# A gated delta-net block with FFN on one core: first norm and gates moved among the slots, FFN moved into the attention's buffers, substitution steps moved behind x0

## The chip, the core and the metric

The kernel runs on one core of a Trainium2 chip. The metric is the device time of one execution in microseconds. TensorE is called PE, VectorE DVE, ScalarE ACT, GpSimd POOL and SyncE SP; SP issues all DMAs here. Everything is computed in float32.

## What is computed

The input x has 4 sequences of 1024 tokens with 256 features. The reference, cut to what matters:

```python
x = x + layernorm(attn(layernorm(x)))
x = x + layernorm(ffn(layernorm(x)))

# attn: gated delta rule, 32 value heads on 16 key heads of width 128, chunks of C = 64 tokens
mixed = silu(conv4(x @ W_qkv.T)); q, k, v = split(mixed); q, k = l2norm(q), l2norm(k)
beta  = sigmoid(x @ W_b.T)
g     = -exp(A_log) * softplus(x @ W_a.T + dt_bias);  gc = cumsum(g) in each chunk
decay = exp(gc_i - gc_j) for i >= j
A     = -((beta*k) @ k.T * decay) below the diagonal
T     = inverse(I - A)                       # unit lower triangular, 64 x 64
u, kcd = T @ (beta*v), T @ (beta*k*exp(gc))
for each chunk in order, with the state S (128 x 128 per head):
    v_new = u - kcd @ S
    out   = (q*exp(gc)) @ S + (q @ k.T * decay) @ v_new
    S     = S*exp(gc_last) + (k*exp(gc_last - gc)).T @ v_new
attn = (out * rsqrt(mean(out^2)) * norm_w * silu(x @ W_z.T)) @ W_out.T

# ffn: weights are looked up, w = lut[idx] with 16 entries; inner width 688
ffn = (silu(x @ Wg.T) * (x @ Wu.T)) @ Wd.T
```

## The kernel before

A *tile* is 128 tokens: the same chunk of two sequences (names `ab`). A *unit* of the attention is one tile for one *group* of 4 value heads (2 key heads). There are 32 tiles and 8 groups, so 256 units. Eight units make a *super*; there are 32 supers, four to a group.

**Head.** The first norm runs over four blocks of eight tiles (L207): load x, statistics (`layer_norm_stats`, DVE with the root on POOL), scale (`normed_to`), transpose on PE into `xnT` (all normed tokens, features on the partitions), and multiply by the weights of beta and g into `ba`. Then the gates of all heads are computed on 128x1024 tensors (L225 to L256), and for each group `dk` (exponentials of the sums, the sums, beta, the decay of a chunk) goes to DRAM as `dk_d`, the sums by rows as `rows_d` (L258 to L280). `load_qk` brings `dk` back when its group begins.

**Slots.** The attention is a software pipeline whose order on PE, ACT, DVE and POOL is written out by hand: every engine executes its instructions in the order of the program. Slot s, from -21 to 255, runs a list of names from `SLOTS`, chosen by the index iq = (s + 21) mod 8:

- `B`, `A`: one channel of q/k (for units 21 slots ahead) and one of v (4 slots ahead): PE products `pp` into a two-bank PSUM tile (two of these exist, shared by `A`, `B` and the state product `pu`), ACT gives the first tap into `cv`, DVE the other three taps (L439), ACT the SiLU.
- `n`, `s`: norms of q and k; scores with the decay (`kkq`, `dc`, `lT`, `aT`).
- `v1`: one step of `invert`, a forward substitution over 31 columns for all 32-row diagonal blocks of a super: a product into `rank` (L579) and a subtraction from `v` (L580), both DVE with two inputs in SBUF. The 31 steps of a super are dealt out over eight slots. `b` (`build`) makes the other blocks; `expand` loads the result into `ue`, `ae`.
- `N0` to `N3`, then `O3`, `O4`, `J` one slot later: the steps of a unit. `N0` transposes v (`pv`) into x0; `N1` multiplies by the state (`pkqs`), and DVE adds the result to x0 (L694); `N2` applies the inverse to x0 (PE `px`, L703), ACT and DVE evacuate (`xs`, `yg`), POOL decays the state (L720); `O3` gives the output of the chunk (`po`, `core`); `O4` is the state product `pu` and its addition to S (L747); `J` squares on ACT.
- `Z`, `T`, `U`: the output projection (`project_out`) of a unit five slots back: `pz` on PE, SiLU on ACT, two products on POOL (L783, L785), transposes, `pout`, and the sum over groups through `acc_d` in DRAM.

After `O4` one step of the lookup of the FFN's weights runs on POOL (`pieces`, L300 and L304).

**Tail.** After slot 255 five projections run one after another; the pools of the attention close; the FFN (L931) loads its weights and goes over four blocks of eight tiles: second norm, gate and up (`pgu`), product `hT`, down (`py`), last norm, store.

Of the kernel before, what the change touches and what calls it, by code (L numbers as in the profile page):

```python
# [2 lines left out]

# [55 lines left out]
def bc(ap, shape):  # L59
    return ap.to_broadcast(shape)  # L60
# [3 lines left out]
def delta_net_ffn_kernel(  # L64
# [43 lines left out]
    ones = filled("ones", 1.0, BS)  # L108
# [18 lines left out]
    nc.sync.dma_start(cw, convw)  # L127
    nw = const.tile([P, 1], F32, name="nw")
    nc.sync.dma_start(nw, normw)
    lutb = const.tile([P, NLUT], F32, name="lutb")  # L130
    nc.sync.dma_start(lutb, lut.to_broadcast([P, NLUT]))
# [24 lines left out]
    dk_d = dram.tile([NG, P, DK], F32, name="dk_d")  # L156
    rows_d = dram.tile([NG, 2, NTILE * HG, C], F32, name="rows_d")

    def rows_of(t, n0, n, p, ab):

        r = (2 * p + ab) * S + n0 * C
        return t[r : r + n * C, :].rearrange("(n t) d -> t n d", t=C)

    def tile_rows(xt, p, ab):

        return xt.rearrange("q (n p) d -> q n p d", p=NPAIR)[ab * C : (ab + 1) * C, :, p, :]
# [15 lines left out]

    def transposed(dst, srcs):

        for kc in range(KC):
            pt = bank("pt")
            for i, src in enumerate(srcs):
                T_.transpose(pt[:, i * P : (i + 1) * P], src[:, kc * P : (kc + 1) * P], ident)
            to = dst(kc)
            A.copy(to, pt if len(to.shape) == 2 else pt.rearrange("p (n b t) -> p n b t", n=2, b=B))  # L190


    with tc.tile_pool(name="pre", bufs=2) as pre, tc.tile_pool(name="gates", bufs=1) as gp:
        wb = gp.tile([P, KC, 2 * NV], F32, name="wb")
        nc.sync.dma_start(wb, wba.rearrange("(c p) n -> p c n", p=P))
        dtr = gp.tile([P, NV], F32, name="dtr")
        nc.sync.dma_start(dtr, dtb.to_broadcast([P, NV]))
        nea = gp.tile([P, NV], F32, name="nea")
        nc.sync.dma_start(nea, alog.to_broadcast([P, NV]))
        ba = gp.tile([P, NTILE, 2 * NV], F32, name="ba")  # L200
        sel = []
        for ab in range(2):
            rows = gp.tile([P, P], F32, name=f"sel{ab}")
            G_.memset(rows, 0.0)
            G_.memset(rows[ab * C : (ab + 1) * C, :], 1.0)
            sel.append(rows)
        for s in range(NSB):  # L207
            xt = pre.tile([P, SB, HID], F32, name="xt")
            for p in range(NPAIR):
                for ab in range(2):  # L210
                    nc.sync.dma_start(tile_rows(xt, p, ab), rows_of(x, 4 * s, 4, p, ab))
            mv, r = layer_norm_stats(pre, lambda i: xt[:, i, :], SB, "a")
            for i in range(SB):
                normed_to(xt[:, i, :], xt[:, i, :], mv, r, i)
            for h in range(2):
                at = H + (4 * s + 2 * h) * C
                transposed(
                    lambda kc: xnT[:, kc, :, at : at + BT].rearrange("p b (n t) -> p n b t", n=2),
                    [xt[:, 4 * h + i, :] for i in range(4)],
                )  # L220
            pg = bank("pg")
            for i in range(SB):
                by_rows(pg[:, i * 64 : (i + 1) * 64], lambda kc: wb[:, kc, :], s * SB + i)
            A.copy(ba[:, s * SB : (s + 1) * SB, :], pg.rearrange("p (t n) -> p t n", n=64))
        full = [P, NTILE, NV]  # L225
        gl = gp.tile(full, F32, name="gl")
        beta = gp.tile(full, F32, name="beta")
        A.activation(beta, ba[:, :, 0:NV], AF.Sigmoid)
        A.activation(nea, nea, AF.Exp)
        V.tensor_scalar_mul(nea, nea, -1.0)  # L230
        y = gp.tile(full, F32, name="y")
        u = gp.tile(full, F32, name="u")
        w = gp.tile(full, F32, name="w")
        d = gp.tile(full, F32, name="d")
        l = gp.tile(full, F32, name="l")
        V.tensor_tensor(y, ba[:, :, NV:], bc(dtr.unsqueeze(1), full), ALU.add)


        A.activation(u, y, AF.Abs)
        A.activation(u, u, AF.Exp, scale=-1.0)  # L240
        V.tensor_scalar_add(w, u, 1.0)
        A.activation(l, w, AF.Ln)
        V.tensor_scalar(d, w, -1.0, LOG1P_SERIES / 2, ALU.add, ALU.max)
        V.reciprocal(d, d)
        V.tensor_mul(l, l, d)
        V.tensor_mul(l, l, u)
        V.tensor_scalar(w, u, -1 / 4, 1 / 3, ALU.mult, ALU.add)
        V.tensor_mul(w, w, u)
        V.scalar_tensor_tensor(w, w, -1 / 2, u, ALU.add, ALU.mult)
        V.scalar_tensor_tensor(w, w, 1.0, u, ALU.add, ALU.mult)  # L250
        V.tensor_sub(l, l, w)
        V.scalar_tensor_tensor(l, u, LOG1P_SERIES, l, ALU.is_gt, ALU.mult)
        V.tensor_add(l, l, w)
        V.tensor_scalar_max(y, y, 0.0)
        V.tensor_add(y, y, l)
        V.tensor_tensor(gl, y, bc(nea.unsqueeze(1), full), ALU.mult)  # L256
        nth = NTILE * HG
        for g in range(NG):  # L258
            hs = slice(g * HG, (g + 1) * HG)
            dk = pre.tile([P, DK], F32, tag="dk", name="dk")  # L260
            ps = bank("pgate")
            for i, lhs in enumerate((triu, slow)):
                T_.matmul(ps[:, i * nth : (i + 1) * nth], lhsT=lhs, rhs=gl[:, :, hs], start=True, stop=True)
            A.activation(dk[:, 0 : 2 * nth], ps[:, 0 : 2 * nth], AF.Exp)
            V.tensor_copy(dk[:, 2 * nth : 3 * nth], ps[:, 0:nth])
            ps = bank("pgate")
            for ab in range(2):
                T_.matmul(
                    ps[:, ab * nth : (ab + 1) * nth], lhsT=sel[ab], rhs=gl[:, :, hs], start=True, stop=True
                )  # L270
            el = dk[:, 4 * nth : 6 * nth].rearrange("p (t a h) -> p a t h", a=2, h=HG)
            A.activation(el, ps[:, 0 : 2 * nth].rearrange("p (a t h) -> p a t h", a=2, h=HG), AF.Exp)
            V.tensor_copy(dk[:, 3 * nth : 4 * nth].rearrange("p (t h) -> p t h", h=HG), beta[:, :, hs])
            ps = bank("prow")
            T_.transpose(ps[:, :P], dk[:, 2 * nth : 3 * nth], ident)
            rows = pre.tile([P, P], F32, tag="rows", name="rows")
            A.copy(rows, ps[:, :P])
            for ab in range(2):
                nc.sync.dma_start(rows_d[g, ab], rows[:, ab * C : (ab + 1) * C])
            nc.sync.dma_start(dk_d[g], dk)  # L280
# [27 lines left out]
    with ExitStack() as main:  # L308
# [17 lines left out]
        for name in ("ue", "ae"):  # L326
            zeroed[name] = [w1.tile(h4, F32, tag=f"{name}{i}", name=name) for i in range(NZ)]
            for t in zeroed[name]:
                G_.memset(t, 0.0)
# [3 lines left out]
        for t in pads:  # L333
            G_.memset(t, 0.0)
# [706 lines left out]
```

## Time and profile before

| | |
|---|---|
| median of 3 runs | 4435.06 us (4429.75 to 4438.18) |
| execution profiled | 4434.46 us, of which span 4432.7 us |
| granted clock of PE in it | 0.968 |
| first norm done, by its last products | 55 us |
| first channel product (slot -21) | 109.7 us |
| first transposes of v (slot 0) | 254 us |
| last unit's output (slot 255) | 4017 us |
| first instruction of the FFN's second norm | 4097.5 us |

The profile is one execution. A row of a stage table gives start:end, length, and the busy time of PE, of PE's weight loads, of DVE, ACT and POOL in it, each with its number of instructions, then the granted clock of PE, the DMA share and GB/s. Matmuls are pipelined, so a busy PE is not a PE at its peak. A line of the timeline gives start, length, engine, line, operation, what is written and read, and in brackets the idle time of the engine ahead of it and what ended it. Every matmul in float32 shows as two instructions.

### The profile page before, as it was taken

The numbers are of one execution on the slowest core, as the hardware profiler recorded it, in microseconds if no ns is written. First come the engines' busy times: TensorE is split into PE (matmuls) and PEld (weight loads), VectorE is DVE, ScalarE is ACT, GpSimd is POOL, SyncE is SP. The second block draws the span as 40 slices with busy tenths as digits, with TensorE's granted clock in tenths as the row PEclk, the third lists the DMA queues.
The fourth block names the chain that finished last, engine by engine and source line by source line (L and its number), as shares of the span: only waits on it lengthen the run. The fifth ranks groups of instructions, "written<-read, shape, count | busy, mean of one in ns | idle before, by whom it ended". The sixth has DMA issues, their size and how long they took to land.

```text
span 4432.7 us, 79363 instructions
## 1 busy us (share of the span) xinstructions
PE 4021.3 (91%) x26664; PEld 2876.3 (65%) x26664; DVE 3514.5 (79%) x6641; ACT 2646.0 (60%) x6573; POOL 2069.1 (47%) x1752
## 2 busy tenths in 40 slices
PE   3679999999999999999999999999999999995888
PEld 3456766676767766677667676776766666673444
DVE  4788888888888888888888888889888888861442
ACT  2466666666666666666666666666666666662111
POOL 2545554655555555554455555555453334331221
PEclk7899999999999999999999999999999999997999
DMA  3444444544454444444444445444444444432110
GB/s 94 114 116 110 106 120 118 133 117 114 129 135 125 118 121 132 114 116 127 126 130 118 115 127 135 125 116 118 126 119 117 123 126 120 102 84 72 36 33 19
DMA packets 1052418, 492.70 MB, mean 111 GB/s; under 512 B 729824, under 2 KB 951152, under 8 KB 1052016
## 3 DMA queue, kind: packets, MB, share of 16 engines
q1 hardware_dynamic: 1052016, 487.64, 42.0%
q8 instruction: 216, 3.54, 0.3%
q14 instruction: 186, 1.52, 0.1%
HBM read 267.66 MB, written 219.69 MB: 110 GB/s over the span
## 4 chain that ended last, share of the span: by engine, by line
PE 59%; DVE 24%; issue 6%; ACT 6%; POOL 3%; DMA 2%; SPq 1%; DVEq 0%; POOLq 0%; ACTq 0%
PE pp L422 13%; DVE cv L439 8%; PE pout L796 7%; PE pz L142 7%; PE pkqs L683 7%; PE px L703 4%; DVE rank L579 4%; PE pu L740 4%; PE po L703 3%; PE pgu L963 3%; PE py L975 2%; DVE v L580 2%; PE kkq L545 2%; PE pto L789 2%; PE pv L670 1%
## 5 line engine op out<-in xcount | busy, mean ns | idle before, releaser
L439 DVE SCALAR_TENSOR_TENSOR cv<-pp,cw,cv 128x512 f32<-128x512 f32 x1536 | 1148.8, 748 | 356.6 <-ACT cv L436 327.2
L783 POOL TENSOR_TENSOR zs<-zs,rr 128x512 f32<-128x512 f32 x256 | 266.4, 1041 | 1586.6 <-ACT zs L781 1577.6
L436 ACT ACTIVATE cv<-pp,cw 128x512 f32<-128x512 f32 x512 | 350.7, 685 | 489.3 <-PE pp L422 489.3
L580 DVE TENSOR_TENSOR v<-v,rank 128x31 f32<-128x31 f32 (+15 forms) x992 | 555.0, 559 | 34.1
L422 PE MATMUL pp<-xnT,wq 128*128 128x262 f32 x2048 | 532.1, 402 | 43.8 <-DVE cv L439 35.1
L796 PE MATMUL pout<-wo,oT 128*128 128x256 f32 x2048 | 512.0, 395 | 8.1 <-ACT oT L791 8.1
L422 PEld LDWEIGHTS pp<-xnT,wq 128*128 128x128 f32 x2048 | 372.7, 192 | 217.1 <-issue 59.6
L422 PE MATMUL pp<-xnT,wv 128*128 128x262 f32 x2048 | 502.5, 387 | 6.1 <-DVE cv L439 6.1
L142 PE MATMUL pz<-wzs,xnT 128*64 128x512 f32 x2048 | 488.8, 598 | 4.7 <-DVE ac L801 3.8
L579 DVE TENSOR_TENSOR rank<-v,lb 128x31 f32<-128x31 f32 (+15 forms) x992 | 468.2, 472 | 24.5 <-DMA lb<-ltd 18.8
L683 PE MATMUL pkqs<-S,qku 128*64 128x256 f32 x3840 | 476.8, 387 | 4.2 <-DVE core L727 2.5
L720 POOL TENSOR_TENSOR S<-S,dkm 128x1024 f32<-128x1024 f32 x224 | 436.2, 1947 | 26.0 <-PE pkqs L683 26.0
L703 PE MATMUL px<-x,ue 128*128 128x128 f32 x2048 | 296.1, 289 | 157.5 <-issue 102.2
L703 PEld LDWEIGHTS px<-x,ue 128*128 128x128 f32 x2048 | 266.9, 196 | 258.0 <-issue 147.7
L422 PEld LDWEIGHTS pp<-xnT,wv 128*128 128x128 f32 x2048 | 381.4, 190 | 74.1 <-issue 13.4
L796 PEld LDWEIGHTS pout<-wo,oT 128*128 128x128 f32 x2048 | 388.2, 200 | 56.3 <-ACT oT L791 10.0
L683 PEld LDWEIGHTS pkqs<-S,qku 128*64 128x64 f32 x3840 | 249.2, 136 | 201.4 <-issue 51.0
L732 ACT ACTIVATE junk<-core 128x128 f32<-128x128 f32 x1024 | 318.8, 311 | 66.7 <-DVE core L727 38.4
L785 POOL TENSOR_TENSOR zs<-zs,core 128x512 f32<-128x512 f32 x256 | 328.4, 1283 | 20.1
L708 ACT ACTIVATE xs<-px 128x512 f32<-128x512 f32 x256 | 154.4, 603 | 237.5 <-PE px L703 237.4
L740 PE MATMUL pu<-yg,kt 64*128 64x256 f32 x1920 | 272.2, 402 | 15.4 <-DVE cv L439 14.0
L300 POOL TENSOR_SCALAR lt<-lx,lutb 128x344 f32<-128x344 int32 (+2 forms) x210 | 276.6, 1317 | 16.9
(166 smaller groups left out, 7081.7 us busy)
## 6 DMA issues: line engine op xcount, KB each, us to landing
qkd<-qk SPq DMA_DIRECT2D x256, 256.0 KB, 2.5
qku<-qkd SPq DMA_DIRECT2D x256, 256.0 KB, 2.9
dc<-rows_d SPq DMA_DIRECT2D x256, 128.0 KB, 3.4
ltd<-lT SPq DMA_DIRECT2D x128, 256.0 KB, 2.5
atd<-aT SPq DMA_DIRECT2D x128, 256.0 KB, 2.8
ae<-atd SPq DMA_DIRECT2D x512, 64.0 KB, 2.6
acc_d<-ac SPq DMA_DIRECT2D x256, 128.0 KB, 2.2
ac<-acc_d SPq DMA_DIRECT2D x224, 128.0 KB, 2.6
```

Source lines behind the costliest of these rows:

```text
L142: T_.matmul(ps[ab * C : (ab + 1) * C, :], lhsT=xnT[:, kc, 2 * p + ab, H + n * C : H + (n + 1) * C], rhs=rhs(kc), start=kc == 0, stop=kc == ...
L422: T_.matmul(ps[:, 2 * p : 2 * p + 2, : H + BT], lhsT=wt[:, kc, :], rhs=xnT[:, kc, 2 * p : 2 * p + 2, c0 : c0 + H + BT], start=kc == 0, sto ...
L436: A.activation(cv, ps[:, :, H : H + BT], AF.Copy, scale=cw[:, ch, H : H + 1])
L439: V.scalar_tensor_tensor(cv, ps[:, :, i : i + BT], cw[:, ch, i : i + 1], cv, ALU.mult, ALU.add)
L579: V.tensor_tensor(t, bc(v[:, 0 : j + 1, j : j + 1], sh), bc(lb[:, j : j + 1, j + 1 :], sh), ALU.mult)
L580: V.tensor_tensor(v[:, 0 : j + 1, j + 1 :], v[:, 0 : j + 1, j + 1 :], t, ALU.subtract)
L683: T_.matmul(as4(ps)[ab * C : (ab + 1) * C, two, :], lhsT=qk[:, m, j, ab, :], rhs=S_[:, ab, two, :], start=True, stop=True,)
L703: T_.matmul(as4(ps)[:, h, :], lhsT=w[:, h, :], rhs=src[:, h, :], start=True, stop=True)
L720: G_.tensor_tensor(flat, flat, bc(decay, [P, 2 * HG, P]), ALU.mult)
L740: T_.matmul(as4(pu[:, ab])[:, two, :], lhsT=kt[half, m, :], rhs=yg[half, two, :], start=True, stop=True)
L785: G_.tensor_tensor(zs, zs, k.cores.pop(u), ALU.mult)
L796: T_.matmul(pp[:, :HID], lhsT=oT[:, h, :], rhs=wo[:, h, :], start=h == 0, stop=h == HG - 1)
```

## The change

1. **First norm by units.** `first_norm(v)` does four tiles; eight of them. Unit 0 runs ahead of slot -21, unit v ends in slot v - 22. Its x tiles lie in the buffers of `core`, its weights in that of `kt`. The loads of x come first in SP's queue, those of constants and weights behind them.
2. **Gates by groups.** `gates(g, t0, t1)` does one group, in the `dk` tile in SBUF itself; there is no `dk_d`. Group 0 is done in two parts in slots -21, -20 and -13, -12. The gates of group g + 1 are done in eight steps within the slots of group g, at its slots 3, 5, 9, 10, 13 (end of the slot) and 4, 8, 12 (behind `s`). Beta is 1 / (1 + exp(-b)) instead of a sigmoid on ACT; the sum over a chunk uses 64 rows of `ones` instead of two selecting matrices.
3. **Taps in the start-up.** In slots below -4 with odd iq, the taps of channel `B` are made by ACT into buffers of `vt` and added by POOL, instead of DVE.
4. **Memsets** of `ue`, `ae` and `pads` move into slot -20; `pieces` begins at slot 0.
5. **Substitution.** In `SLOTS`, the `v1` between `J` and `O4` and the one behind `O4` go behind `N1` (x0), as `v2`, with `Z` next; `rank` has one buffer instead of two.
6. **FFN in the attention's buffers.** Tiles of `sq`, `dc`, `lT`, `aT`, `qk0`, `qk1`, `pads`, `vt`, `cv`, `x0` and `core` are taken for x, sums, weights, `hT` and outputs. The FFN works by units of four tiles. The second norm of units 0 to 3 and the loads of weights run in slots 240 to 255 (`early_ffn`). After the last slot gate_up of unit 0 is interleaved with the six remaining projections, two at a time; then, for each unit, down(v) and gate_up(v + 1) are interleaved with the last norm of v - 1 and the second norm of v + 2. The last unit is stored tile by tile.

The core of the diff:

```diff
+        def first_norm(v):
+            xt = []
+            for n in range(2):
+                t = t4("core", OUT_LAG)...
+                for ab in range(2):
+                    nc.sync.dma_start(t[ab * C : (ab + 1) * C], chunk_rows(x, 2 * v + n, ab))
+                xt += [t[:, i, :] for i in range(2)]
+            yield
+            mv, r = layer_norm_stats(w2, lambda i: xt[i], 4, "b")
+            for i in range(4):
+                normed_to(xt[i], xt[i], mv, r, i)
+            yield
...
+            yield
+        def gates(g, t0, t1):
...
+            V.tensor_tensor(th(y), ba[:, t0:t1, NV + g * HG : NV + (g + 1) * HG], ..., ALU.add)
+            yield
+            A.activation(u, y, AF.Abs)
+            A.activation(u, u, AF.Exp, scale=-1.0)
+            A.activation(th(beta), ba[:, t0:t1, hs], AF.Exp, scale=-1.0)
+            yield
+            V.tensor_scalar_add(w, u, 1.0)
+            V.tensor_scalar_add(beta, beta, 1.0)
+            V.reciprocal(beta, beta)
+            yield
+            A.activation(l, w, AF.Ln)
+            yield
...
             cv = sc.tile([P, B, BT], F32, tag="cv", name="cv", bufs=3)
             A.activation(cv, ps[:, :, H : H + BT], AF.Copy, scale=cw[:, ch, H : H + 1])
+            if far:
...
+            else:
+                for i in reversed(range(H)):
+                    t = w1.tile([P, 512], F32, tag="vt", name="tap", bufs=2 * HG)...
+                    A.activation(t, ps[:, :, i : i + BT], AF.Copy, scale=cw[:, ch, i : i + 1])
+                    G_.tensor_add(cv, cv, t)
...
-                t = sc.tile([P, BS * BS // 4], F32, tag="rank1", name="rank1", bufs=2)
+                t = sc.tile([P, BS * BS // 4], F32, tag="rank1", name="rank1")
...
         SLOTS = [
-            "A v1 O3 s N0 v1 T n J O4 v1 N1 Z v1 B n N2 U n s",
-            "A v1 O3 N0 v1 T J v1 O4 N1 r Z v1 B N2 q s U",
-            "A v1 O3 N0 v1 T J v1 O4 v1 N1 Z s v1 B N2 n U",
+            "A v1 O3 s N0 v1 T n J O4 N1 v1 Z v1 B n N2 U n s",
+            "A v1 O3 N0 v1 T J O4 N1 v2 r Z v1 B N2 q s U",
+            "A v1 O3 N0 v1 T J O4 N1 v2 Z s v1 B N2 n U",
             "b A O3 N0 T J O4 N1 Z s B N2 U b",
-            "v1 A b O3 s N0 v1 T n J O4 v1 N1 Z v1 B n N2 v1 U n s",
-            "A v1 O3 N0 v1 T J v1 O4 v1 N1 r Z v1 B N2 q s v1 U",
-            "A v1 O3 N0 v1 T J v1 O4 v1 N1 Z s v1 B N2 n v1 U",
-            "A v1 O3 N0 v1 T J v1 O4 v1 N1 Z s v1 B N2 v1 U",
+            "v1 A b O3 s N0 v1 T n J O4 N1 v2 Z B n N2 v1 U n s",
+            "A v1 O3 N0 v1 T J O4 N1 v2 r Z v1 B N2 q s v1 U",
+            "A v1 O3 N0 v1 T J O4 N1 v2 Z s v1 B N2 n v1 U",
+            "A v1 O3 N0 v1 T J O4 N1 v2 Z s v1 B N2 v1 U",
         ]
...
+                    if name == "s" and s >= 0 and s % SLOTS_G in (4, 8, 12):
+                        ahead_gates(s)
                     if name == "O4":
-                        next(pieces, None)
+                        if s >= 0:
+                            next(pieces, None)
...
+                if s < 0:
+                    started_up(s)
+                elif s % SLOTS_G in (3, 5, 9, 10, 13):
+                    ahead_gates(s)
+                if s >= EARLY:
+                    next(early, None)
...
+            rest = [gated] + [project_out(*unit) for unit in units[len(units) - OUT_LAG :]]
+            part = gate_up(0)
+            while rest or part:
+                for gen in rest[:2]:
+                    if next(gen, END) is END:
+                        rest.remove(gen)
+                if part and next(part, END) is END:
+                    part = None
+            for v in range(NU):
+                nxt = gate_up(v + 1) if v + 1 < NU else None
+                side = [ended(v - 1, range(4))] if v else []
+                if 4 <= v + 2 < NU:
+                    side.append(prepared(v + 2))
+                    next(side[-1])
+                side = chain(*side)
+                if nxt:
+                    next(nxt)
+                for i in range(4):
+                    down(v, i)
+                    next(side, None)
+                    if not nxt:
+                        drain(ended(v, [i]))
+                while nxt and next(nxt, END) is not END:
+                    next(side, None)
+                drain(side)
```

`prepared(v)` is the second norm of a unit (load, statistics, scale and add on POOL, statistics, scale, transposes), `ended(v, tiles)` the last norm with the store, `gate_up(v)` six product tiles with SiLU and product, `down(v, i)` one tile of the last product.

## The prediction

> **What bounds the kernel now.** I read the page first (busy shares, slices, chain), then the table of stages, because one average hides that this program has a serial head, a long steady part and a serial tail; then the waits of TensorE in the steady part, and one slot of it in the timeline.
>
> ```profile
> span 4432.7 us, 79363 instructions
> PE 4021.3 (91%) x26664; PEld 2876.3 (65%) x26664; DVE 3514.5 (79%) x6641; ACT 2646.0 (60%) x6573; POOL 2069.1 (47%) x1752
> PE 59%; DVE 24%; issue 6%; ACT 6%; POOL 3%; DMA 2%; SPq 1%; DVEq 0%; POOLq 0%; ACTq 0%
> ```
>
> PE bounds most of it, but a quarter of the chain is DVE. The stages (length, busy time of each engine, granted clock, DMA share):
>
> ```profile
> 0.00:57.00 57.00, 28.14 (x320) 22.05 (x320) 28.91 (x98) 14.24 (x24) 21.87 (x39) 0.88 0.38 82
> 57.00:109.70 52.70, 14.92 (x73) 12.96 (x73) 25.13 (x31) 15.64 (x31) 5.17 (x9) 0.62 0.33 105
> 109.70:254.00 144.30, 95.00 (x461) 60.85 (x462) 98.71 (x182) 65.14 (x98) 76.56 (x66) 0.82 0.45 124
> 254.00:4017.00 3763.00, 3561.58 (x24873) 2613.79 (x24871) 3228.59 (x5987) 2491.20 (x6303) 1883.83 (x1541) 0.99 0.45 119
> 4017.00:4080.50 63.50, 37.96 (x111) 19.67 (x109) 3.27 (x10) 10.78 (x22) 11.50 (x10) 0.73 0.07 21
> 4080.50:4118.20 37.70, 3.50 (x16) 3.23 (x17) 17.10 (x57) 1.64 (x3) 9.74 (x12) 0.55 0.66 171
> ```
>
> First norm (57 us), gates (52.7 us) and 21 start-up slots (144.3 us) precede slot 0 at 254; 256 slots take 3763 us (14.7 each) with PE 95% busy; then come six output projections one after another (PE 60% busy, clock 0.73), the load of the FFN (PE 3.5 us of 37.7) and the FFN, to 4432.7. In the steady part nearly all idle time of PE lies ahead of one product, the substitution's result applied to x0:
>
> ```profile
> PE px L703 <- issue: 94.9, 40, 3.1
> PE px L703 <- ACT cv L436: 37.6, 28, 1.4
> ```
>
> I count a super's eight slots by their index into SLOTS, 0 to 7. Slots 88 to 90 have the indices 5, 6 and 7:
>
> ```profile
> 1562.66:1578.67 16.01, 13.39 (x85) 9.67 (x84) 15.52 (x29) 10.11 (x25) 8.69 (x8) 1.00 0.39 87
> 1578.67:1595.31 16.64, 14.32 (x101) 10.53 (x100) 16.32 (x28) 10.45 (x27) 11.58 (x9) 1.00 0.29 76
> 1595.31:1610.84 15.53, 14.10 (x100) 10.61 (x99) 15.15 (x30) 8.23 (x24) 5.79 (x4) 1.00 0.62 171
> ```
>
> DVE (third pair) is busy nearly throughout and PE idles 2.6, 2.3 and 1.4 us; in the four slots that follow PE has no gap. So DVE binds three slots of eight, PE five. The timeline of slot 89 shows how:
>
> ```profile
> 1585.78 1.22 DVE L747 TENSOR_TENSOR S<-pu,S 128x1024 f32<-128x1024 f32 x1
> 1586.55 1.04 POOL L783 TENSOR_TENSOR zs<-zs,rr 128x512 f32<-128x512 f32 x1 [2.87 <-ACT zs L781]
> 1586.92 0.95 DVE L579 TENSOR_TENSOR rank<-v,lb 128x252 f32<-128x252 f32 x1
> 1587.67 1.32 POOL L785 TENSOR_TENSOR zs<-zs,core 128x512 f32<-128x512 f32 x1
> 1587.90 1.37 DVE L580 TENSOR_TENSOR v<-v,rank 128x252 f32<-128x252 f32 x1
> 1588.95 2.07 POOL L720 TENSOR_TENSOR S<-S,dkm 128x1024 f32<-128x1024 f32 x1
> 1589.19 1.11 DVE L694 SCALAR_TENSOR_TENSOR x<-pkqs,dkm,x 128x128 f32<-128x128 f32 x4
> 1589.73 1.13 PE L703 MATMUL px<-x,ue 128*128 128x128 f32 x8 [2.07 <-issue]
> ```
>
> A pair of substitution instructions (L579, L580) stands between the state's update and x0. It takes 2.3 us; the pair ahead of the update, one column block smaller, took 0.84. px waits 2.07 us for x0.
>
> **Head.** Removed: norm and gates as stages of their own. The first unit of norm (4 tiles) is: x lands at about 5 us (its loads now lead SP's queue; before they stood sixth and the first statistics ran at 8.9), statistics 2.1, rsqrt on POOL 0.24 + 1.67, four scalings 1.35, transposes and copies 3, gate products at the cold clock 3: slot -21 starts at about 16.5 instead of 109.7. Put among the slots: seven more units (four loads each on SP, issued two units ahead), in slots -21 to -15. DVE's queue holds statistics and scalings of a unit back to back, so it stands 2 us for POOL's rsqrt: 2.1 + 2.1 + 1.35 = 5.6 us, plus 2.3 for the taps in every second slot, 6.8 per slot, 48 us for seven; before, these slots took 29 (first channel products at 109.7 and 138.8). +19. Group 0's gates come in two passes, each a DVE, ACT, DVE, ACT, DVE, PE, ACT chain with up to four table loads of 1.28 and some fifteen small DVE instructions: 8 us each, +16. Half the channels of the slots before -4 give their taps to ACT (3 x 0.69) and POOL (3 adds; nearest rows 1.04 to 1.28); that is 24 DVE taps of 0.748, 18 us, but mostly in slots that waited on a chain anyhow: -4. Slot 0: 16.5 + 144.3 + 19 + 16 - 4 = 192, so **-62 us**. Check by DVE's sum: 98.7 - 18 + 27 (norm) + 6 (gates) = 114 us in 175 us, 65%, as loose as the 68% before. Ends: -85 (chains overlap better) and -30 (every chain adds up). The memsets (5 us, POOL, slot -20), the constants' loads now behind x on SP and the index lookup that now starts at slot 0 and ends at 223 lie beside other work; the last would cost only if it ran past slot 240.
>
> **Tail.** Full-speed rows of the chain: gate and up of a unit 20.93, down 11.94, transposes of a unit 2. Now: six projections beside gate_up(0): PE work 6 x (0.6 + 1.73) + 5 x 1.72 + 20.9 = 43.5; the six product tiles run out after seven of some eighteen rounds, and the single buffer of zs keeps a chain of 0.6 + 1.04 + 1.26 + transposes per projection, about 6 us: 52. Transposes of units 2 and 3: 4. Seven rounds of 32.9: 230; transposes of units 4 to 7: 8; last down 12; its copy, statistics, rsqrt, scaling, add and store 9.5; waits of PE for hT, with statistics and scalings (18 us of DVE per 33) in the same queue: 10. Sum 326 from 4017, against 415.7. The work moved into slots 240 to 255 (two units in full, two in part: DVE 10 us each where DVE is busy 25.7 of 50, PE 2 us each where PE has no gap, 32 loads on SP ahead of expand's, 0.3 to 0.6 us each against a lead of one slot): +6. **-84 us**; ends -100 and -60.
>
> **Gates in the slots**, seven groups. DVE: two reciprocals (6.55 us for 1024 columns, so 0.85 for 128), ten two-input instructions of 0.23, four of 0.15: 4.7 us, of which 3.4 fall in slots 6 and 7, where DVE binds. PE: four products and a transpose, 1.9 us in slots 1 and 2, where PE binds, plus a wait for one of four PSUM banks, of which this step takes three. ACT: one more table load (1.28) and 2.5 us, covered (60% busy). I take 2.5 of DVE and 1.5 of PE as uncovered: 4 x 7 = **+28 us**; ends +10 and +50. SP gets two stores of rows per group and loses the load of dk; both lie a slot or more ahead of their use.
>
> **Substitution behind x.** Two pairs leave the place ahead of x0 in slots 2 and 5 to 7, one in 0, 1 and 4. x0 comes 3 us earlier in slot 5 (0.7 + 2.4), px 2.6. What is late next: the taps of channel B hold the two-bank tile that the state product pu needs in the next slot. Their end stands 1.3 to 2.8 us ahead of pu(6), pu(7), pu(0), and 0.06 us ahead of pu(2). The moved pairs then run beside POOL's L783, L785 and L720. The lines above give the price: L580 took 1.37 beside L785, and 0.42 in the pair before. The Trainium skill (SBUF — State Buffer, Who interferes with whom) says that a VectorE instruction with two SBUF inputs and a GpSimd one that reads SBUF exclude each other for the whole instruction. This speaks against the change: four instructions behind x0 meet 1.04 + 1.27 + 1.90 = 4.2 us of POOL where two met 1.5 us of delay before. By the rule to the letter each such slot pays up to 2.7 us more, 8.1 in slots 5 to 7, 28 supers: +227 us. The trace says less: L300 also reads SBUF, yet the pair beside it in the same slot (1591.4) took 0.52 and 0.42, so only POOL's two-input instructions count; and as PE comes earlier so do L783 and L785, before the pairs. Walking slots 5, 6, 7, 0, 1 with these rows leaves DVE 0.7, 0.2, 1.1, 0.6 and 1.1 us later than before, PE 2.1 and 1.1 earlier at pu(6) and pu(7), level at pu(0), and at pu(2) about 1 later, of which slots 2 to 4 (2.8 us and more of idle DVE) keep some 0.4. **+10 us**; ends -60 and +60 (the full lock belongs to a rival). The second rank buffer is free: each step already waits for the one before through v.
>
> **Sum** against the execution profiled: 4432.7 - 62 - 84 + 28 + 10 = 4325 of span; 1.8 lie around the span (4434.5), and the median of the runs is 0.6 above that: **4327 us**.
>
> **Rivals.** (1) The px waits go and nothing takes their place: 2.4 us for each of 28 supers, instead of +0.4: 4250. For it: 4.9 us of px wait per super; against: DVE idles only 2 us over slots 5 to 1. (2) The head hardly shrinks: POOL's tap adds have two SBUF inputs and lock DVE out where the first inversion runs, and the norm's chains add to the gates': -25 instead of -62: 4364. (3) Slower: the lock. In slots 5 to 7 both pairs wait for L785 and L720 whole, DVE grows by 5.5 us per super, and since pu waits for the taps PE gets all of it: 4317 + 154 = 4471. It decides from (62 + 84 - 28) / 28 = 4.2 us per super. For it: the 1.37; against: PE's lead moves POOL too. (4) Gains and losses cancel.
>
> **Numbers.** Own forecast 0.62; (1) 0.15; (2) 0.15; (3) 0.06; (4) 0.02. A measurement here can tell 0.2%, 9 us. Faster is 0.62 + 0.15 + 0.15 = 0.92, same 0.02, slower 0.06. Range 4255 to 4392: the unknown ends (25, 18, 20, 55, taken as independent, 66) about 4327, which takes in (2) and nearly (1).
>
> **What would show it.** Slot 0 (first transposes of v) at 175 to 215 us; last slot to end 310 to 340 us, PE over 90% in it; px waits in slots 5 to 7 below 1.5 us per super and waits of pu for cv in their place; L579 and L580 above 32 us per super together if the lock grows. Wrong if slot 0 is past 230, if the tail keeps gaps of 10 us, or if the 256 slots differ from 3763 by more than 90.

## The result, and the profile after

The changed kernel takes 4538.74 us (median of 4 runs, 4536.55 to 4541.54), against 4435.91 for the kernel before beside it: a ratio of 1.0234, 95% interval 1.0217 to 1.0252. It is slower by about 103 us, where 4327 was predicted. Rival (3) had the right sign and the right mechanism; its 4471 still held the head's -62 and the gates' 28.

The page of the changed kernel, its span, busy times and chain:

```profile
span 4539.8 us, 79714 instructions
PE 4090.8 (90%) x26673; PEld 2894.3 (64%) x26673; DVE 3634.5 (80%) x6747; ACT 2681.3 (59%) x6656; POOL 2116.6 (47%) x1810
DVE 45%; PE 35%; ACT 11%; issue 6%; POOL 1%; DMA 1%; SPq 1%; DVEq 0%; ACTq 0%; POOLq 0%
```

The chain has changed owner: DVE carries 45% of it (24% before), PE 35% (59%). PE has about as many products as before (26673 and 26664 records) but is busy 69 us longer. The stages (length, busy times, granted clock, DMA share): start-up slots, slots 0 to 255, and the seven rounds of the FFN:

```profile
30.70:251.70 221.00, 125.84 (x761) 86.32 (x760) 129.87 (x266) 103.03 (x169) 78.80 (x77) 0.76 0.32 87
251.70:4226.00 3974.30, 3664.15 (x24946) 2650.48 (x24945) 3395.19 (x6206) 2518.83 (x6370) 1959.42 (x1615) 0.97 0.43 114
...
4290.00:4522.00 232.00, 232.00 (x706) 120.70 (x704) 85.80 (x215) 38.83 (x78) 47.43 (x68) 1.00 0.11 28
```

The balance, counted between first transposes of v: slot 0 at 251.7 instead of 254.0 (-2); from slot 0 to slot 255 3965.2 instead of 3754.5 (+211); from slot 255 to the end 323.0 instead of 424.3 (-101). Together +107, the difference of the two spans. The tail did what it should, the head gave nothing, and the slots lost twice what the tail brought. By the two rows of the slots, PE idles 310 us in them instead of 201 and is busy 3664 instead of 3562, at a granted clock of 0.97 instead of 0.99: half of the loss is waiting, half is longer busy time for about as many products (24946 and 24873).

Where PE waits, from the list of waits of the whole run (total us, times, longest):

```profile
PE pto L790 <- DVE yg L712: 124.9, 105, 1.9
PE pu L741 <- DVE cv L434: 81.5, 111, 2.5
PE px L704 <- DVE x L695: 8.2, 5, 3.7
```

The waits of px for x0 are nearly gone. In their place stand the wait of pu for the taps that the prediction named (14.0 in 17 before), and one of pto for yg (7.0 in 10 before), which waits in the same DVE queue: DVE is late behind x0 now instead of ahead of it. A slot with index 7 in the timeline (start, duration) shows what makes it late:

```profile
914.68 1.04 POOL L784 TENSOR_TENSOR zs<-zs,rr 128x512 f32<-128x512 f32 x1 [12.69 <-ACT zs L782]
...
915.29 0.70 DVE L580 TENSOR_TENSOR rank<-v,lb 128x247 f32<-128x247 f32 x1
...
915.80 1.32 POOL L786 TENSOR_TENSOR zs<-zs,core 128x512 f32<-128x512 f32 x1
916.03 1.37 DVE L581 TENSOR_TENSOR v<-v,rank 128x247 f32<-128x247 f32 x1
...
917.09 2.06 POOL L721 TENSOR_TENSOR S<-S,dkm 128x1024 f32<-128x1024 f32 x1
917.43 1.99 DVE L580 TENSOR_TENSOR rank<-v,lb 128x240 f32<-128x240 f32 x1
...
925.17 1.23 PE L741 MATMUL pu<-yg,kt 64*128 64x256 f32 x4 [0.73 <-DVE cv L434]
```

The two pairs behind x0 stand beside the three products of POOL, and the first three of their four instructions end 0.27 to 0.28 us after a POOL product does: they take 0.70, 1.37 and 1.99 us, where the pair ahead of x0 in the same slot took 0.41 and 0.42. The taps follow them, and pu follows the taps. Over the whole run, before and after (count, busy us, mean ns; the lines of the kernel have moved by one):

```profile
L579 DVE TENSOR_TENSOR rank<-v,lb 128x31 f32<-128x31 f32 (+15 forms) x992 | 468.2, 472 | 24.5 <-DMA lb<-ltd 18.8
L580 DVE TENSOR_TENSOR v<-v,rank 128x31 f32<-128x31 f32 (+15 forms) x992 | 555.0, 559 | 34.1
...
L580 DVE TENSOR_TENSOR rank<-v,lb 128x31 f32<-128x31 f32 (+15 forms) x992 | 596.9, 602 | 47.9 <-DMA lb<-ltd 40.2
L581 DVE TENSOR_TENSOR v<-v,rank 128x31 f32<-128x31 f32 (+15 forms) x992 | 575.4, 580 | 34.1
```

Divided by 32 supers, the pair of lines takes 36.6 us per super, against 32.0 before. The 1984 instructions can also be sorted by what POOL runs when they start, each measured against the time that the fastest 5% of its shape take in the kernel before. With POOL idle (1262 of them) they take 0.01 us more than that, beside one of POOL's `tensor_scalar` (175) 0.08 us, and beside one of its two-input products 0.4 to 1.4 us in the mean. Beside the decay of the state, the longest product, 132 start, against 47 before.

### The profile page after: what moved, and what is told of

Its sections match the earlier page's. It is cut to its first block, busy times and chain, and to the rows that moved or that the text cites. A ratio compares the mean times of both kernels' runs of the same rounds, so it can differ in the third digit from the quotient of the medians.

```text
span 4539.8 us, 79714 instructions
## 1 busy us (share of the span) xinstructions
PE 4090.8 (90%) x26673; PEld 2894.3 (64%) x26673; DVE 3634.5 (80%) x6747; ACT 2681.3 (59%) x6656; POOL 2116.6 (47%) x1810
## 4 chain that ended last, share of the span: by engine, by line
DVE 45%; PE 35%; ACT 11%; issue 6%; POOL 1%; DMA 1%; SPq 1%; DVEq 0%; ACTq 0%; POOLq 0%
DVE cv L434 13%; DVE rank L580 10%; PE pp L416 7%; DVE v L581 6%; PE pz L140 4%; PE pout L797 4%; PE pgu L986 4%; PE pkqs L684 3%; DVE S L748 3%; DVE x L695 2%; DVE core L728 2%; PE pu L741 2%; PE px L704 2%; DVE yg L712 2%; PE py L1002 2%
## 5 line engine op out<-in xcount | busy, mean ns | idle before, releaser
L434 DVE SCALAR_TENSOR_TENSOR cv<-pp,cw,cv 128x512 f32<-128x512 f32 x1512 | 1130.9, 748 | 357.2 <-ACT cv L430 328.5
L580 DVE TENSOR_TENSOR rank<-v,lb 128x31 f32<-128x31 f32 (+15 forms) x992 | 596.9, 602 | 47.9 <-DMA lb<-ltd 40.2
L581 DVE TENSOR_TENSOR v<-v,rank 128x31 f32<-128x31 f32 (+15 forms) x992 | 575.4, 580 | 34.1
L684 PE MATMUL pkqs<-S,qku 128*64 128x256 f32 x3840 | 516.3, 413 | 16.2 <-DVE ac L802 8.9
L797 PE MATMUL pout<-wo,oT 128*128 128x256 f32 x2048 | 500.7, 388 | 28.1 <-DVE yg L712 26.5
L140 PE MATMUL pz<-wzs,xnT 128*64 128x512 f32 x2048 | 492.7, 602 | 14.0 <-ACT x L675 11.2
L797 PEld LDWEIGHTS pout<-wo,oT 128*128 128x128 f32 x2048 | 377.2, 194 | 80.4 <-DVE yg L712 27.8
L684 PEld LDWEIGHTS pkqs<-S,qku 128*64 128x64 f32 x3840 | 268.2, 147 | 243.9 <-issue 67.7
L444 ACT ACTIVATE qk<-cv 128x512 f32<-128x512 f32 x256 | 161.4, 630 | 412.2 <-DVE cv L434 386.0
L741 PE MATMUL pu<-yg,kt 64*128 64x256 f32 x1920 | 301.5, 437 | 82.6 <-DVE cv L434 81.5
L704 PE MATMUL px<-x,ue 128*128 128x128 f32 x2048 | 280.9, 280 | 15.6 <-DVE x L695 8.2
L189 POOL TENSOR_SCALAR lt<-lx,lutb 128x344 f32<-128x344 int32 (+2 forms) x210 | 282.4, 1345 | 16.8
```

The lines of the kernel that those rows point to most:

```text
L140: T_.matmul(ps[ab * C : (ab + 1) * C, :], lhsT=xnT[:, kc, 2 * p + ab, H + n * C : H + (n + 1) * C], rhs=rhs(kc), start=kc == 0, stop=kc == ...
L434: V.scalar_tensor_tensor(cv, ps[:, :, i : i + BT], cw[:, ch, i : i + 1], cv, ALU.mult, ALU.add)
L580: V.tensor_tensor(t, bc(v[:, 0 : j + 1, j : j + 1], sh), bc(lb[:, j : j + 1, j + 1 :], sh), ALU.mult)
L581: V.tensor_tensor(v[:, 0 : j + 1, j + 1 :], v[:, 0 : j + 1, j + 1 :], t, ALU.subtract)
L684: T_.matmul(as4(ps)[ab * C : (ab + 1) * C, two, :], lhsT=qk[:, m, j, ab, :], rhs=S_[:, ab, two, :], start=True, stop=True,)
L704: T_.matmul(as4(ps)[:, h, :], lhsT=w[:, h, :], rhs=src[:, h, :], start=True, stop=True)
```

## The experiments

All ratios are to the kernel before, run beside it. "Slot 0" and "tail" (from slot 255) are from each profile; "per group" is the mean length of the second to seventh group of 32 slots.

| | time, us | ratio, 95% interval | slot 0 | per group | tail |
|---|---|---|---|---|---|
| before | 4435.1 | 1 | 254.0 | 480.5 | 424.3 |
| changed | 4538.7 | 1.0234 (1.0217 to 1.0252) | 251.7 | 507.7 | 323.0 |
| changed, order of before | 4422.4 | 0.9975 (0.9965 to 0.9984) | 248.4 | 491.9 | 321.9 |
| before, new order | 4557.5 | 1.0278 (1.0263 to 1.0294) | 259.5 | 497.2 | 423.3 |
| before, no POOL products | 4262.7 | 0.9611 (0.9595 to 0.9628) | 258.1 | 461.4 | 401.3 |
| the same, new order | 4251.2 | 0.9588 (0.9574 to 0.9603) | 256.8 | 459.1 | 407.2 |
| head: POOL's queue | 4402.4 | 0.9933 (0.9918 to 0.9948) | 229.6 | 490.7 | 323.5 |
| and taps on DVE | 4397.6 | 0.9921 (0.9906 to 0.9936) | 222.9 | 491.9 | 321.9 |
| and the ring cut | 4387.7 | 0.9901 (0.9886 to 0.9916) | 216.9 | 492.2 | 321.9 |
| gates: products last | 4429.1 | 0.9992 (0.9985 to 0.9998) | 251.1 | 492.7 | 321.8 |
| gates: in DVE's slack | 4400.2 | 0.9923 (0.9907 to 0.9940) | 252.8 | 488.3 | 323.3 |
| gates: spread | 4385.9 | 0.9893 (0.9876 to 0.9909) | 251.3 | 486.8 | 321.9 |
| all mended | 4369.3 | 0.9852 (0.9836 to 0.9869) | 219.7 | 488.6 | 323.1 |
| gates ahead of lb | 4343.9 | 0.9802 (0.9785 to 0.9819) | 217.5 | 484.9 | 321.8 |

**The order of the slots alone.** Theory: the place behind x0 is the price. Rival: the order costs nothing, the gates and the early FFN do. First the changed kernel with the old order of steps, then the kernel before with the new one:

```diff
-            "A v1 O3 N0 v1 T J O4 N1 v2 Z s v1 B N2 v1 U",
+            "A v1 O3 N0 v1 T J v1 O4 v1 N1 Z s v1 B N2 v1 U",
...
```

> The changed kernel with only the hand-written order of the slots put back to that of before (substitution steps ahead of x0 again in the same places); first norm, gates, FFN as changed. Theory (behind x0 each substitution instruction waits for one POOL instruction with two SBUF inputs, DVE gets 4 to 5 us more per super and hands it to PE through the taps ahead of pu): about 4400 us, 135 below the changed kernel, L580+L581 back to 32 us per super. Rival (the order costs nothing; the 211 us of the slots come from the gates and from SP's and POOL's extra work): 4510 to 4550.

> The kernel before with only the new order of the slots. Theory: slower by 4.3 us per super, 31 supers, so about +135: 4570 us, with the px waits gone and waits of pu for the taps in their place. My recorded forecast for this part was +10, 4445; the rival that px waits simply go says 4360.

The changed kernel gets 116 us faster with the old order (L580 and L581 back to 31.7 us per super), and the kernel before gets 123 us slower with the new one (36.7 per super). So the order costs about 120 us whatever stands around it; the rival falls. The second buffer of `rank` plays no part: the first of these runs has one, the other two. The two parts add up: 11.4 us per group from all else and 16.7 from the order make 28.1, and the changed kernel has 27.2.

**Is it POOL?** Both runs leave the same three POOL products out, one in the old order and one in the new:

```diff
-            G_.tensor_tensor(zs, zs, bc(k.rr[u // 4][:, u % 4, :].unsqueeze(2), h4), ALU.mult)
...
-            G_.tensor_tensor(zs, zs, k.cores.pop(u), ALU.mult)
+            k.cores.pop(u)
...
-                    G_.tensor_tensor(flat, flat, bc(decay, [P, 2 * HG, P]), ALU.mult)
```

> The kernel before without three products on POOL: zs by the root, zs by the core's output, and the decay of the state (left out of the computation). Baseline for the next run. Both theories: substitution steps near their shortest, 21 us per super instead of 32, and the kernel some 100 to 250 us faster than before, as DVE gets 11 us per super back and binds three slots of eight by about 5 us.

> As the run before (the same three products on POOL left out) but with the new order of the slots. Theory (POOL's products are what makes the new order slow): no more than 20 us slower than that run, or faster. Rival (it is the order itself: four substitution instructions ahead of the taps that pu waits for, whatever POOL does): slower by about 100 us or more.

This is the run that settles it. Without the products the new order is 11.6 us *faster* than the old; with them it is 123 slower. It is not the order of DVE's queue as such. (Both runs also free DVE of 8 us per super, which could hide a small price of the order itself.) The two groups in the new order without the products (busy us, mean ns):

```profile
L580 DVE TENSOR_TENSOR v<-v,rank 128x31 f32<-128x31 f32 (+15 forms) x992 | 395.2, 398 | 34.0
L579 DVE TENSOR_TENSOR rank<-v,lb 128x31 f32<-128x31 f32 (+15 forms) x992 | 364.7, 368 | 30.7 <-DMA lb<-ltd 23.0
```

Their sum is 23.7 us per super, and in the old order too (397.9 and 361.7 us): the place makes no difference once these three products are out of the way. (I expected 21; the products that are left on POOL, those of `scores` and of the lookup, still meet some.)

**The head.** From here on every run is the changed kernel with the old order. Theory: POOL's queue holds the first root and keeps DVE's scalings waiting. The head of the changed kernel in the timeline:

```profile
21.22 2.86 POOL L249 TENSOR_SCALAR wo<-wo,nw 128x1024 f32<-128x1024 f32 x1 [17.66 <-DMA lx<-in_gidx]
...
25.56 1.38 DVE L169 TENSOR_SCALAR core<-core,mvb,rb 128x256 f32<-128x256 f32 x4 [18.46 <-POOL rb L165]
...
46.67 3.94 POOL L442 TENSOR_TENSOR cv<-cv,tap 128x512 f32<-128x512 f32 x3
46.74 4.35 DVE L169 TENSOR_SCALAR core<-core,mvb,rb 128x256 f32<-128x256 f32 x4 [1.47 <-POOL rb L165]
...
61.33 7.37 DVE L169 TENSOR_SCALAR core<-core,mvb,rb 128x256 f32<-128x256 f32 x4 [1.47 <-POOL rb L165]
```

`load_o(0)` stands ahead of the first unit's root in the program, so POOL waits 17.7 us for the weights of the projection (the profile names another load of the same queue) before it computes the root that DVE has waited 18.5 us for. Later the four scalings take 4.35 us beside the taps' additions and 7.37 beside the memsets, instead of 1.38.

```diff
-            G_.tensor_scalar_mul(wo, wo, nw)
...
+            for t in (*zeroed["ue"], *zeroed["ae"], *pads):
+                G_.memset(t, 0.0)
             next(norms_1[0])
...
+            if s + LQ == 10:
+                G_.tensor_scalar_mul(w_o[0], w_o[0], nw)
```

> The changed kernel with the order of the slots of before, and two things taken out of POOL's way in the head: the scaling of the first wo by norm_w is done in slot -11 instead of ahead of the first root, and the memsets of the padded tiles come first on POOL instead of in slot -20. Theory (the head lost its gain to POOL's queue: a DMA wait ahead of the first root, and work on POOL that keeps DVE's scalings waiting): slot -21 starts at about 17 us instead of 30.4, slots -21 to -15 take some 8 us less; slot 0 at 225 to 230, time 4400. Rival (the first unit is bound by its loads and the chain of its steps): slot -21 still at 28 or later and the time within 9 us of the kernel with the old order alone, 4422.

```diff
-                    gens["B"] = channel(supers[nq], iq // 4, iq % 4, 0 if s < -LV and iq % 2 else 1)
+                    gens["B"] = channel(supers[nq], iq // 4, iq % 4, 1)
```

> As the run before, and all taps of the start-up slots on DVE again instead of every second channel on ACT and POOL. Theory (POOL's tap additions lock DVE's statistics and scalings, and POOL's root and additions and ACT's taps wait in a ring): slots -21 to -15 fall by another 15 us or more, slot 0 at 205 to 215, time about 4385. Rival (the seven slots are bound by the chain of the norm itself): slot 0 within 5 us of the run before, or later, since DVE has 24 taps of 0.75 more.

The first edit did what it should: slot -21 starts at 16.6 instead of 30.4 (16.5 was predicted for the changed kernel), the slot with the memsets falls from 16.3 to 9.8, slot 0 comes at 229.6. The second fell short: the seven norm slots take 79.4 us, 3.0 less, where 15 were expected, and slot 0 comes 7 earlier. The times (4402.4 and 4397.6) have overlapping intervals. POOL explains the start, and little of the length of the norm slots. In the timeline these slots were a ring of queues in program order: the channel products, cv, taps, SiLU, then the copies of the transposes behind the SiLU on ACT, then the gate products, and the next channel products behind those on PE. So I cut it:

```diff
+            yield
             pg = bank("pg")
...
+                for v in (s + LQ + 1, s + LQ + 3, s + LQ + 2):
+                    if v < len(norms_1):
+                        next(norms_1[v])
```

> As the run with the taps on DVE, and the norm's last step cut in two: the transposes and their copies of the next unit stand at the start of a slot, ahead of the channel, and only the gate products at its end; loads and statistics come one unit earlier. Theory (the seven norm slots are a ring through queues in program order: channel products 3.5 us at the cold clock, cv 0.7, taps 2.3, SiLU 0.6, the copies of the transposes 1.1 behind it on ACT, gate products 2.25, channel products: 10.4 per slot): without the copies in it a slot is about 7 us, slots -21 to -15 take 50 to 58 us instead of 79.5, and the time falls by 20 to 28, to about 4372. Rival (statistics, root and scaling on DVE and POOL bind the slots): no change of more than 9 us.

The seven slots fall from 79.4 to 68.4 us, but slot -21 starts 2.6 later with one unit more ahead of it, and slot 0 comes at 216.9, 6 us earlier. That is a part of what I expected, and the two times differ by 10 us with intervals that just overlap. The five slots behind the first two take 4.0 to 10.7 us now, against 10.0 to 13.3; the first two, with group 0's first gates in them, take 14.5 and 14.8. What is left between 216.9 and the 192 predicted was not taken apart further.

**The gates.** Without the order, 11.4 us per group are left where 4 were predicted. They are the gates': in the run with the old order the fourteen slots of a group up to their last step take 12.0 us more than before, the other eighteen 0.7 less. Slot 12 alone takes 19.3 us instead of 13.0, and there the gates' products are followed by a wait of 2.9 us of the output projection. Theory: PSUM banks.

```diff
-            sums = [bank("pgate")[:, :n] for _ in range(2)]
+            sums = [ps[:, 2 * n : 3 * n], bank("pgate")[:, :n]]
...
-                    if name == "s" and s >= 0 and s % SLOTS_G in (4, 8, 12):
+                    if name == "s" and s >= 0 and s % SLOTS_G in (4, 8):
...
-                elif s % SLOTS_G in (3, 5, 9, 10, 13):
-                    ahead_gates(s)
+                else:
+                    for _ in range((3, 5, 9, 10, 12, 13).count(s % SLOTS_G)):
+                        ahead_gates(s)
```

> The changed kernel with the order of the slots of before, and of the gates only the step with products moved: from behind N2 of slot 12 of a group to that slot's end, behind the output projection, and in two PSUM banks instead of three. Theory (the step takes the banks that the output projection needs, and PE waits 2.9 us for DVE's yg and then runs at the lower clock): slot 12 falls from 19.3 to about 15 us, 3 to 5 us per group, 4390 to 4400. Rival (the gates' cost is DVE's work in the slots bound by DVE): within 9 us of 4422.

This failed: 4429.1 us, 7 more than with the old order alone. Slot 12 fell to 14.8, and slot 13 rose from 14.0 to 19.0. In the trace ACT now loads its tables twice (1.28 us each) ahead of the exponentials of `pgate`, DVE waits 3.1 us with the copy of the sums and has core and the taps queued behind it, and the transposes pto start just as that copy ends. I took it that the products with their exponentials and their copy hold up whatever slot binds on PE, and moved everything: DVE's steps to where DVE was thought to have time, the products to where PE has.

```diff
-                    if name == "s" and s >= 0 and s % SLOTS_G in (4, 8):
+                    if name == "s" and s >= 0 and s % SLOTS_G in (4,):
...
-                    for _ in range((3, 5, 9, 10, 12, 13).count(s % SLOTS_G)):
+                    for _ in range((3, 5, 6, 7, 7, 9, 10).count(s % SLOTS_G)):
```

> As the run before, but all steps of the gates moved: DVE's steps to the ends of slots 5 and 7 of a group, where PE binds and DVE idles, the logarithm to the end of slot 6, the products to the end of slot 9 and the rows to the end of slot 10, where DVE binds. Theory (11.5 us per group are collisions and not work): 3 to 5 us per group are left, 4360 to 4375. Rival (the work itself, with its table loads, costs it wherever it stands): not below 4400.

The time, 4400.2, is short of the 4360 to 4375 expected. Slots 9 to 13 went back to within 0.7 us of the kernel before, but slot 8 rose to 23.4 us (16.8 before): all thirteen instructions behind the logarithm ran there in a row, ahead of the taps, and the channel products waited 4.4 us for these. Next they were cut into four parts:

```diff
             V.tensor_mul(l, l, d)
+            yield
...
+        GATES_AT = {(1, ""), (4, "s"), (4, ""), (5, ""), (6, "Z"), (6, ""), (7, "O4"), (7, "Z"), (9, ""), (10, "")}
...
+                    if s >= 0 and (s % SLOTS_G, name) in GATES_AT:
```

> The changed kernel with the order of the slots of before and the gates' steps as in the last run of them, but the thirteen DVE instructions behind the logarithm in four parts in slots 6 and 7 of a group instead of all at once ahead of the taps of slot 8. Theory (the 6.6 us left in slot 8 are the channel products waiting for taps behind those thirteen): slot 8 falls from 23.4 to 16.8 or so, 1 to 3 us per group of gates are left, time about 4355. Rival (DVE's 4.6 us have to be paid wherever they stand): the 6.6 us show up in slots 6 and 7, time 4395 or more.

Between theory and rival: 4385.9 us, and 6.3 us per group are left. Slot 8 fell to 15.3, but slot 7 rose from 14.6 to 18.7, because the last part, placed behind x0, met POOL again: three of its instructions took 1.87, 1.01 and 1.32 us instead of 0.29. The changed kernel's fault, made again in my own mend. Then all of it together, with the last nine instructions ahead of O4 in slot 7:

```diff
-        GATES_AT = {(1, ""), (4, "s"), (4, ""), (5, ""), (6, "Z"), (6, ""), (7, "O4"), (7, "Z"), (9, ""), (10, "")}
+        GATES_AT = {(1, ""), (4, "s"), (4, ""), (5, ""), (6, "Z"), (7, "A"), (7, "T"), (7, "O4"), (9, ""), (10, "")}
```

> The changed kernel with all of the above: the order of the slots of before, wo scaled later, memsets first, taps of the start-up on DVE, the norm's last step cut, and the gates spread as in the last run of them but with the last nine instructions behind the logarithm in slot 7 ahead of O4, where no POOL product of the slot runs, instead of behind x0. Theory (the 4 us that slot 7 of a group still paid are the same exclusion by POOL's products: 1.87, 1.01 and 1.32 for instructions of 0.29): slot 7 back from 18.7 to about 15, groups 482 to 484, slot 0 at 217, tail 322: about 4330, 0.977 of before. Rival (the work itself costs 4 us in slot 7): groups at 486 to 488, 4355 to 4360.

A miss by 39 us, and an instructive one. Slot 7 took 22.7 us. From its timeline:

```profile
1790.35 0.19 DVE L584 TENSOR_TENSOR rank<-v,lb 128x31 f32<-128x31 f32 x1 [2.78 <-DMA lb<-ltd]
...
1794.05 1.26 POOL L790 TENSOR_TENSOR zs<-zs,core 128x512 f32<-128x512 f32 x1
1794.15 1.31 DVE L345 SCALAR_TENSOR_TENSOR dkm<-dkm 128x128 f32<-128x128 f32 x1
1795.27 1.94 POOL L725 TENSOR_TENSOR S<-S,dkm 128x1024 f32<-128x1024 f32 x1
1795.49 1.87 DVE L346 TENSOR_TENSOR dkm<-dkm,nea 128x128 f32<-128x128 f32 x1
...
1800.20 2.04 PE L708 MATMUL px<-x,ue 128*128 128x128 f32 x8 [6.39 <-DVE x L699]
```

The first substitution step of a super waits 2.8 us for its lb from DRAM. The gates stood behind it in DVE's queue, so they came 2.8 us late, into POOL's products; then every DVE instruction with two SBUF inputs waited for one POOL product after another, the next pair of substitution too, and px waited 6.4 us. The last run moves the gates ahead of that wait:

```diff
-        GATES_AT = {(1, ""), (4, "s"), (4, ""), (5, ""), (6, "Z"), (7, "A"), (7, "T"), (7, "O4"), (9, ""), (10, "")}
+        GATES_AT = {(1, ""), (4, "s"), (4, ""), (5, ""), (6, "O3"), (6, "N0"), (7, "O3"), (7, "N0"), (9, ""), (10, "")}
```

> As the run before, but the thirteen DVE instructions of the gates stand behind O3 and N0 of slots 6 and 7 of a group: in slot 6 in the time in which DVE idles, in slot 7 ahead of the first substitution step, which waits 2.8 us for its lb from DRAM, instead of behind it. Theory (in the run before that wait pushed seven instructions with two SBUF inputs beside POOL's products, each waited for one of them, and x0 came 6.4 us late): slot 7 falls from 22.7 to 15 or so, slots 7 and 8 together from 35.7 to 32, groups to 482 to 485, time 4335 to 4345. Rival (4.6 us of DVE work cost it in these slots wherever they stand): groups at 486 or more, 4355 or more.

Slot 7 is at 14.6, slots 7 and 8 take 31.5 together (31.4 before), the groups 484.9. The time, 4343.9, is within the expectation, and this version beats both kernels: 0.9802 of before, interval 0.9785 to 0.9819. Its chain is PE's again (58%, with DVE at 25%).

## Why the prediction was wrong, point by point

- **Substitution behind x, predicted +10, measured +116 and +123.** The step that failed: "as PE comes earlier so do L783 and L785, before the pairs". They don't. In the slot shown above the first pair starts 0.6 us after POOL's first product, and three of the four instructions then last until a product is over. The mechanism was in the prediction, with its row (1.37 beside L785) and the rule of the Trainium skill (SBUF — State Buffer, Who interferes with whom). The rule to the letter gave +227, the walk +10; the runs lie halfway. In the trace the rule holds for POOL's two-input products and, as the prediction said, hardly for its `tensor_scalar`, which reads SBUF too (0.08 us). The rule's figure was too high in slots 5 to 7: measured against the fastest as above, in the mean of slots 16 to 239, the substitution there loses 10.5 us per super, 6.9 before, so 3.6 more and not 8.1; slot 1, which the figure left out, loses 2.5 more, and slot 2 1.0 less. DVE's growth, 36.6 against 32.0 us per super, is what rival (3) was to be known by, though its mark, "above 32", was the kernel's own figure before; its 5.5 us per super is close to the 4.6 measured. Its chance, 0.06, was the error: the end that the nearest row and the rule both pointed to was written off by a walk whose order of events nothing in the trace had shown.
- **pu waits for taps.** Right: 81.5 us in 111 waits, 14.0 in 17 before. px's waits went, as said. What was missed is the clock: it was 0.97 over the slots, 0.99 before, and PE was busy 4090.8 us, 4035.6 with the old order and 4005.8 in the last run. That the gaps lower it is inferred from where it is low: between 875 and 980 us PE idles 11.0 us at 0.90, in the 14 us ahead of that it has no gap, at 1.00.
- **Gates in the slots, predicted 4 per group, measured 11.4.** The work was sized nearly right (0.95, 0.29 and 0.21 us an instruction for 0.85, 0.23 and 0.15), and in the last run all that is left, 484.9 - 480.5 = 4.4 per group, is near the forecast. Mis-sized was the term for collisions: the products' banks and copy in a slot bound by PE, DVE's steps ahead of taps or beside POOL. Over seven groups that is 52 us, of which a better placement recovers 49.
- **Head, predicted -62, measured -2.** Three terms failed. Slot -21 was to start at 16.5 and started at 30.7: POOL's queue was not walked, and `load_o(0)` stood in it (the run without it starts at 16.6). The seven norm slots were to take 48 us as a queue of DVE's, and 8 more with the first pass of the gates, and took 89.8: memsets and taps on POOL are 9 of the difference (88.8 to 79.4 in the runs), the ring through ACT and PE 11 (79.4 to 68.4), and PE's clock (0.76 over the start-up, 0.82 before) may lengthen it. The other 12 were not taken apart. The fourteen slots behind them, with the second pass of the gates, were to take 144.3 - 29 + 8 - 4 = 119 and took 131; this was not taken apart either. Rival (2) named POOL's tap additions as the cause; taking them away moved slot 0 by 7 us only.
- **Tail, predicted -84 with +6 in the slots before it.** Measured -101, and the last group of slots is 14.5 us longer in the run with the old order: -87 in sum. The sum is right partly by luck: the tail was put 12 us too long, the early FFN in the slots 8 us too cheap. The seven rounds with their transposes are 232 us of unbroken PE at full clock; the 10 us allowed for waits of PE weren't needed.
- **The criteria.** Slot 0 past 230 and slots off by more than 90 us were named as marks of a wrong prediction; both came true. The tail, 323 from slot 255 (314 from the end of the slots), lies in the band given. The range 4255 to 4392 was not quite its own sum: 66 about 4327 is 4261 to 4393.

## What to carry to other kernels

An instruction with two inputs in SBUF on DVE is not priced by its duration alone but by what POOL runs at that moment: before moving one, list POOL's two-input products in the slot, and take the row that shows both side by side as the price until the trace shows that they don't meet. In queues in program order, what stands *ahead* of a moved instruction matters as much as what follows it: a wait for a DMA (`load_o` ahead of the root, lb ahead of the gates) pushes everything behind it, on POOL out of the head's gain and on DVE into POOL's products. Small work put into a full pipeline costs its own duration only at the right place; here the same gates, moved about, left between 4.4 and 12.2 us per group.

## What was not expected of the hardware

- The exclusion chains. Where several such DVE instructions stand in a row beside a row of POOL products, each takes about one product's time: 1.31 and 1.87 us beside POOL's 1.26 and 1.94, where the same instructions alone take 0.29. POOL's own products hardly stretch (2.06 us for the decay of the state, whose mean is 1.95).
- x0's additions, which read PSUM, take 1.11 us in that stretch, as they do elsewhere.
- The scalings of the norm (one SBUF tensor and columns) are not spared: 4.35 us instead of 1.38 beside POOL's additions, and 7.37 beside memsets, which read nothing. POOL is the cause: with the memsets moved, the four scalings beside them take 0.41 us each (one took 6.41), and with the taps on DVE so do the three that took 1.35 to 1.42. Which of POOL's accesses they wait for was not tested.
